# Group-norm products on GpSimd with wider stage spacing, a padded ninth tap, and late M products in a fused four-layer convolution kernel

## The chip, the cores and the metric

The kernel runs on one core of a Trainium2 chip. The metric is device time of the program in microseconds, as the median of several runs. The profile records one execution of its own: TensorE's matmuls (PE) and its weight loads (PEld), VectorE (DVE), ScalarE (ACT), GpSimd (POOL) and SyncE's DMA queue (SP).

## The reference

The input x has 4 images of 32 x 32 points and 16 channels. Four layers each add something to x. Three of them (0, 1 and 3 in the reference) are a convolution whose weights differ from point to point and whose result meets every point of the image:

```python
x = x + conv(_gn(x), M, W, G)

# conv, with L = 1
first   = einsum('ijyx,byxc->bijc', Msq, inputs)
shifted = conv3x3(inputs, kernels of all 1024 points x 16 channels)   # (b, i, j, y, x, c)
diff    = relu(inputs[:, None, None] - shifted)
second  = einsum('ijyx,bijyxc->bijc', Wsq, diff)
return first - second
```

`_gn` is a group norm over pairs of channels and the whole image. For each output point (i, j), batch and channel, `shifted` is an image of 1024 values: a product of 144 weights (9 taps by 16 channels) with the image's patches. Together that is a matrix product of 16384 rows by 144 by 4096 columns per layer. Then follow the relu and a weighted sum over the 1024 values.

Layer 2 of the reference is an interval layer: running maxima over a 32 x 32 table, then two steps that add two tables, apply a sigmoid and take a maximum, and a last small product with sigmoid.

## The kernel before

**Phases and steps.** The four images are two groups g of two (GB = 2). The kernel's three convolution layers times two groups make six phases, in the order (layer 0, g 0), (layer 0, g 1), (layer 1, g 0), and so on. While one group is in its phase, the other group's norm, transfers and splits for the next phase are done behind it. The interval layer is done behind phase 3 (for g 0) and phase 4 (for g 1).

A phase is 8 chunks t of 128 output points, and a chunk is 32 steps: 16 channels f times 2 batches b. A step computes for 128 output points and one channel an image of 2 x 512 columns in a pair of PSUM banks. There are four such pairs. `first_part` has 8 matmuls (64 rows of weights, 512 columns), then ScalarE scales the pair in place (L609); `second_part` adds 6 matmuls, then VectorE reads the pair with minimum, multiply by the row of W and sum in one instruction (`junk`, L625). `conv_layer` issues the first part of a step and then the second part of the step before. Weights and images are split into a high and a low part to keep float32's accuracy. The weights' part of that is `prep_parts`.

**Units and weights.** A unit is 4 channels of a chunk, so 8 steps. `load_raw` brings its raw weights (3 slots of 4 x 128 per partition: taps 0 to 3, taps 4 to 7, and the ninth tap), two buffers deep. `prep_parts` is a generator with 8 yields, one part for each step: VectorE masks the high part (`upper`, L175, the tile upper_w), ScalarE halves the ninth tap's weights (L151), GpSimd adds the rest to them on two slices of 32 partitions (L222), GpSimd forms the low parts WL (L224), subtracts the identity from the next unit's weights (`prep`, L185), and forms the differences WD (L212). Then SP's queue gets the next `load_raw`. The tiles of prepared weights are three deep.

**Work behind a phase.** Everything for the next phase is one generator, `behind(phase)`. Each value that it yields is the number of steps until it is resumed; IDLE (0) means: in the next step in which `prep_parts` has little to do. What a phase has not taken after its 256 steps is issued at its end in one go.

`before_conv` is the part that leads from X of the other group to its split images: `group_norm` with its stages (sums, totals of the mean, mean and difference, squares and their sums, totals of the variance, square root, reciprocal and product), a transpose on VectorE (L336), 4 transfers to DRAM (L341), 24 transfers back as shifted patches into the tile `raw` (L351), all on SP's queue, then a pause, and for each batch `split` (VectorE's `upper` of the patches, the tile upper_x; GpSimd's iz; ScalarE's iy), the halving of the ninth tap's patches on ScalarE and VectorE (L151, L154) and the differences iyz on GpSimd (L260). In the norm's totals, VectorE reduces a 32 x 32 transpose (L285, L288), adds four quarters (L294) and transposes back (L299).

`first_terms` multiplies the normed images by M: 128 matmuls (L381), two transposes (L388) and two additions to X (L391), for both groups at once. Its matrix is loaded by `load_first_terms` in two transfers (L371) into a tile with the tag `big`, which the interval layer's tables share. It is done behind phases 0, 2 and 4, after `before_conv`.

`interval_layer` has its own norm, four transposes (L464), scans in two halves each (`running`, L482) with a GpSimd copy between (L490), and then two `step`s of GpSimd additions (L536) and VectorE maxima (L543).

All instructions of an engine run in the order in which they were issued. That order is the one that these generators write out, and the schedule is by hand (`manual_schedule`).

Of the kernel before, what the change touches and what calls it, by code (L numbers as in the profile page):

```python
# [15 lines left out]
P = 128  # L16
B, H, C = 4, 32, 16
NG = 2
# [23 lines left out]
def net_kernel(ctx: ExitStack, tc: tile.TileContext, x, xq, xi, convs, iv_w, iv_b, out):  # L42
# [17 lines left out]

    nc = tc.nc
    ctx.enter_context(tc.manual_schedule())

# [30 lines left out]
    def load_raw(u):  # L96
        if u < n_chunks * NU:
            n = u // NU
            raws[u] = wpool.tile([P, 3, FU, P], F32, tag="raw", bufs=RAWS, name=f"raw_{u}")
            nc.sync.dma_start(raws[u], convs[phases[n // NT][1]][2][n % NT, u % NU])  # L100

    def load_chunk(n):
# [17 lines left out]
    plain = first[:, : PLAIN * 3 * FU * P].rearrange("p (u s f k) -> p u s f k", u=PLAIN, s=3, f=FU)  # L120
    for u in range(PLAIN):
        raws[u] = plain[:, u]
    nc.scalar.dma_start(raws[0][:, :, :F0], convs[0][2][0, 0][:, :, :F0])
    for slot in (0, 2, 1):
        nc.sync.dma_start(raw[:, slot, 0, :RUN], xi[0][:, slot, :RUN])
    load_chunk(0)
    nc.sync.dma_start(raws[0][:, :, F0:], convs[0][2][0, 0][:, :, F0:])
    nc.sync.dma_start(raw[:, :, 1, :RUN], xi[1][:, :, :RUN])
    nc.sync.dma_start(raws[1], convs[0][2][0, 1])


    eps = const.tile([P, 1], F32, name="eps")
# [58 lines left out]
    def prep_parts():  # L191

        for u in range(PLAIN, n_chunks * NU):
            units[u] = [
                wpool.tile([P, 2, FU, P], F32R, tag=tag, bufs=AHEAD + 1, name=f"{tag}_{u}")
                for tag in ("WU", "WL", "WD")
            ] + [wpool.tile([P, FU, P], F32R, tag="W9", bufs=AHEAD + 1, name=f"W9_{u}")]  # L200
            src = raws.pop(u)
            w8 = src[:, :2].rearrange("p s f k -> p s (f k)")
            w9 = src[:, 2]
            WU, WL, WD = (t.rearrange("p s f k -> p s (f k)") for t in units[u][:3])
            W9 = units[u][3]

            def scaled(s):
                nc.scalar.activation(WD[:, s], high[:, s], AF.Copy, scale=-EPS)  # L208

            def difference(s):  # L210
                nc.scalar.copy(WU[:, s], high[:, s])  # L211
                nc.gpsimd.tensor_tensor(  # L212
                    WD[:, s], WD.bitcast(F32)[:, s], WL.bitcast(F32)[:, s], ALU.add
                )

            high = upper(src[:, :2], f"w{u}")
            yield True
            halve(W9, w9, low_w)
            yield False
            scaled(0)  # L220
            for r in (slice(32, 64), slice(96, 128)):
                nc.gpsimd.tensor_tensor(W9[r], W9.bitcast(F32)[r], w9[r], ALU.add)  # L222
            for s in range(2):
                nc.gpsimd.tensor_tensor(WL[:, s], w8[:, s], high[:, s], ALU.subtract)  # L224
            yield False
            scaled(1)
            prep(u + 1)
            yield False
            difference(0)
            yield False  # L230
            difference(1)
            yield False
            load_raw(u + RAWS)
            yield True
            yield True
# [35 lines left out]
    def pair_view(ap):  # L271
        return ap.rearrange("p t (g s) -> p t g s", s=2)

    def group_norm(g, name, dst):


        def sums(src):
            nc.vector.tensor_reduce(
                part[:, : GC // 2], src.rearrange("p t (g s) -> p g t s", s=2), axis=AX.XY, op=ALU.add
            )  # L280

        def totals(name):

            turned = work.tile([P, 32], F32, tag="turned", name=f"turned_{name}")
            nc.vector.transpose(turned, part)  # L285
            by_quarter = work.tile([32, 4], F32, tag="by_quarter", name=f"by_quarter_{name}")
            for q in range(4):
                nc.vector.tensor_reduce(  # L288
                    by_quarter[:, q : q + 1], turned[32 * q : 32 * q + 32], axis=AX.X, op=ALU.add
                )  # L290
            yield 1
            total = work.tile([P, 32], F32, tag="total", name=f"total_{name}")
            for q in range(4):
                nc.vector.tensor_reduce(  # L294
                    total[32 * q : 32 * q + 32, 0:1], by_quarter, axis=AX.X, op=ALU.add
                )
            yield 1
            whole = work.tile([P, 32], F32, tag="whole", name=f"whole_{name}")
            nc.vector.transpose(whole, total[:, 0:1].to_broadcast([P, 32]))  # L299
            return whole[:, : GC // 2]  # L300

        sums(X[g])
        yield 1
        m = yield from totals(f"m{name}")
        mean = work.tile([P, GC // 2], F32, tag="mean", name=f"mean_{name}")
        nc.vector.tensor_scalar_mul(mean, m, 1.0 / (2 * NP))
        yield 1
        xc = work.tile([P, NT, GC], F32, tag="xc", name=f"xc_{name}")
        nc.vector.tensor_tensor(pair_view(xc), pair_view(X[g]), spread(mean), ALU.subtract)
        yield 1  # L310
        sq = work.tile([P, NT, GC], F32, tag="sq", name=f"sq_{name}")
        nc.vector.tensor_tensor(sq, xc, xc, ALU.mult)  # L312
        sums(sq)
        yield 1
        v = yield from totals(f"v{name}")
        yield 2
        yield IDLE
        rstd = work.tile([P, GC // 2], F32, tag="rstd", name=f"rstd_{name}")
        nc.scalar.activation(rstd, v, AF.Sqrt, bias=eps, scale=1.0 / (2 * NP))
        yield 2  # L320
        nc.vector.reciprocal(rstd, rstd)
        nc.vector.tensor_tensor(pair_view(dst), pair_view(xc), spread(rstd), ALU.mult)
        yield 2

    xns = {}
    part = const.tile([P, 32], F32, name="part")
# [2 lines left out]
    def before_conv(g, layer):  # L329
        xn = work.tile([P, NT, GC], F32, tag="xn", bufs=2, name=f"xn_{g}_{layer}")  # L330
        xns[g] = xn
        yield from group_norm(g, f"c{g}{layer}", xn)

        nc.vector.transpose(  # L336
            xt[g][:, :, 1 : 1 + H], xn
        )
        inner = xs[g][:, HP : HP + H * HP].rearrange("p (t r n) -> p r t n", r=ROWS, n=HP)
        for r in range(ROWS):  # L340
            nc.sync.dma_start(inner[:, r], xt[g][GC * r : GC * (r + 1)])  # L341
        yield 2
        xsv = xs[g].rearrange("(b c) n -> c b n", b=GB)
        at = 0
        for slot, row, tap in [(2, row, 8) for row in range(4)] + [
            (tap // 4, tap % 4, tap) for tap in range(8)
        ]:
            for h in range(2):
                off = (HI * h + tap // 3) * HP + tap % 3
                r0 = 64 * h + C * row  # L350
                nc.sync.dma_start(  # L351
                    raw[r0 : r0 + C, slot, :, :RUN], xsv[:, :, off : off + RUN]
                )
            at += 1
            if at % 3 == 0:
                yield 1
        yield 7
        for b in range(GB):
            yield from split(nc.gpsimd, g, b, f"{g}{layer}")
            yield IDLE  # L360
            halve(image(im9[g][:, b], H), image(raw[:, 2, b], HP), low_x)
            for s in range(2):
                difference(nc.gpsimd, g, b, s)
            yield 3
            halve_rest(image(im9[g][:, b], H), image(raw[:, 2, b], HP), low_x)
            yield 1
# [73 lines left out]
    def interval_layer(g):  # L440
# [14 lines left out]
        yield 1  # L455
        nc.gpsimd.memset(r[:R, :, 0:1], 0.0)
        nc.gpsimd.memset(r[:R, H:], 0.0)
        yield from group_norm(g, f"i{g}", xi)

        raw = one[:GC].rearrange("p (j t r) -> p r t j", j=H, r=ROWS)  # L460
        for row in range(ROWS):
# [16 lines left out]
        def running(dst, src):  # L478

            for half in range(2):  # L480
                o = slice(n // 2 * half, n // 2 * (half + 1))
                nc.vector.tensor_tensor_scan(  # L482
                    dst[:, o], resets[:, o], src[:, o], 0.0, op0=ALU.add, op1=ALU.max
                )
                yield 2


        yield from running(one[:, ::-1], other[:, ::-1])
        yield 1
        nc.gpsimd.tensor_copy(table(other), one.rearrange("p (j i) -> p i j", i=H))  # L490
        yield 3
        yield from running(one, other)
# [33 lines left out]
        def step(name, ftp, bias):  # L526
# [20 lines left out]
            nc.scalar.activation(s, s, AF.Sigmoid, bias=bias)  # L547
            for q in range(NQ):
                nc.sync.dma_start(r[R:, QI * q : QI * (q + 1), :], s[GC * q : GC * (q + 1)])
            yield 5  # L550

        yield from right_side("r0", iv["r0"])
        ftp = left("l0", iv["f0"])
# [117 lines left out]
    def behind(phase):  # L671
# [7 lines left out]
        if phase + 1 < len(phases):  # L679
            g1, layer1 = phases[phase + 1]  # L680
            if layer1 == 2:
                yield from interval_layer(g1)
            if g1 == NG - 1:
                mt = load_first_terms(layer1)
            yield from before_conv(g1, layer1)
            if g1 == NG - 1:
                yield from first_terms(layer1, mt)
        if phase == len(phases) - 1:
            yield 4
            nc.sync.dma_start(out[1 - g], X[1 - g])  # L690

# [114 lines left out]
    def rest_of_start():  # L806
# [22 lines left out]
        nc.vector.memset(part, 0.0)  # L829
        zeros(0)  # L830
        xns[0] = work.tile([P, NT, GC], F32, tag="xn", bufs=2, name="xn_00")
        yield from group_norm(0, "c00", xns[0])

    parts = prep_parts()
    for phase in range(len(phases)):
# [77 lines left out]
```

## Time and profile before

| What | Value |
|---|---|
| Median of 3 runs | 2612.41 us (2611.65 to 2615.23) |
| Profiled execution's own time | 2615.03 us |
| Its span | 2613.1 us |
| PE busy | 2570.9 us, 98% |
| DVE busy | 2203.8 us, 84% |
| ACT busy | 2094.6 us, 80% |
| POOL busy | 1812.9 us, 69% |
| DMA, 16 engines, q1 | 200.13 MB, 22.7% |
| Granted TensorE clock | 1.00 |

How to read it: matmuls are pipelined and their ends are modelled, so 98% for PE is not PE at its peak; the chain and the waits show where it stood still. L579 is the line of all the convolution's matmuls. In a row of the groups, the name before the arrow is the tile written, those after it are read; then come partitions x elements, the count, busy us and mean ns, and the idle time of the engine before them. The phases end (last matmul) at 450.4, 874.4, 1305.3, 1745.1, 2190.9 and 2608.7 us.

### The profile page before, as it was taken

What the parts mean: (1) busy time and instruction counts of PE and PEld (TensorE: products, weight loads), DVE (VectorE), ACT (ScalarE), POOL (GpSimd) and SP (SyncE); (2) the same over time, 40 slices, a digit from 0 to 9 for tenths busy, and PEclk for the clock granted to TensorE, in tenths of its full rate; (3) what the DMA queues carried; (4) which work ended last, traced back from release to release, by engine and by line L of the source; (5) the groups of instructions that cost most, each with busy time, mean ns of one, the idle gap of its engine ahead of it and who ended that gap; (6) DMA issues with size and microseconds to landing.
All of it is one profiled execution on the core that took longest, in us unless ns stands there. A gap on an engine that the chain in (4) does not pass through costs nothing.

```text
span 2613.1 us, 56851 instructions
## 1 busy us (share of the span) xinstructions
PE 2570.9 (98%) x21906; PEld 2034.2 (78%) x21906; DVE 2203.8 (84%) x3684; ACT 2094.6 (80%) x2549; POOL 1812.9 (69%) x1446
## 2 busy tenths in 40 slices
PE   8999999999999999999999999999999999999999
PEld 5778888778888778888877777777778778888887
DVE  9977778987787887877798899889889887787877
ACT  4778888788888778888877888877888878888886
POOL 5776666776666676666667887777878676666663
PEclk9999999999999999999999999999999999999999
DMA  3422222312222322222222212311222332222220
GB/s 131 148 82 70 69 70 78 95 68 69 70 77 70 133 87 70 77 71 68 71 68 70 71 58 72 105 69 58 70 72 73 131 95 72 70 77 71 69 70 15
DMA packets 50287, 204.36 MB, mean 78 GB/s; under 512 B 12128, under 2 KB 14048, under 8 KB 49248
## 3 DMA queue, kind: packets, MB, share of 16 engines
q1 hardware_dynamic: 49056, 200.13, 22.7%
q8 instruction: 172, 2.82, 0.4%
q14 instruction: 99, 0.81, 0.1%
q10 hardware_dynamic: 832, 0.58, 0.1%
q0 software_dynamic: 128, 0.02, 0.0%
HBM read 199.19 MB, written 0.98 MB: 77 GB/s over the span
## 4 chain that ended last, share of the span: by engine, by line
PE 88%; DVE 7%; issue 3%; ACT 1%; SPq 0%; DMA 0%; DVEq 0%; POOL 0%; POOLq 0%; ACTq 0%
PE pc L579 87%; DVE junk L625 5%; PE pf L381 1%; DVE upper_w L175 1%; ACT pc L609 0%; SPq L351 0%; DMA raw<-in_g 0%; PE ps_l L504 0%; PE ps_r L517 0%; DVE tables L464 0%; DVE by_quarter_vc L288 0%; DVE acc L638 0%; DVE sq_c L312 0%; DVE sq_i L312 0%; SPq L341 0%
## 5 line engine op out<-in xcount | busy, mean ns | idle before, releaser
L625 DVE SCALAR_TENSOR_TENSOR junk<-pc,WT 128x1024 f32<-128x1024 f32 x1536 | 1877.8, 1223 | 384.6 <-PE pc L579 337.5
L609 ACT ACTIVATE pc<-pc 128x1024 f32<-128x1024 f32 x1520 | 1531.9, 1008 | 468.8 <-PE pc L579 420.4
L579 PE MATMUL pc<-iy,WU 64*128 64x512 f32 x6080 | 970.2, 396 | 28.5 <-DVE junk L625 28.1
L222 POOL TENSOR_TENSOR W<-W,raw 32x512 fp32r<-32x512 f32 x380 | 498.6, 1312 | 708.3 <-issue 614.0
L579 PE MATMUL pc<-iyz,WD 64*128 64x512 f32 x6080 | 962.6, 393 | 2.3 <-ACT pc L609 2.3
L579 PE MATMUL pc<-iz,WL 64*128 64x512 f32 x6080 | 961.1, 392 | 0.0
L579 PEld LDWEIGHTS pc<-iy,WU 64*128 64x128 f32 x6080 | 569.4, 185 | 190.8 <-DVE junk L625 58.0
L579 PEld LDWEIGHTS pc<-iyz,WD 64*128 64x128 f32 x6080 | 575.3, 185 | 142.7 <-ACT pc L609 8.6
L579 PEld LDWEIGHTS pc<-iz,WL 64*128 64x128 f32 x6080 | 576.5, 185 | 135.3
L579 PE MATMUL pc<-im,W 64*128 64x512 f32 x3072 | 619.0, 397 | 0.0
L224 POOL TENSOR_TENSOR WL<-raw,upper_w 128x512 fp32r<-128x512 f32 x380 | 489.0, 1308 | 16.7 <-DVE upper_w L175 2.1
L212 POOL TENSOR_TENSOR WD<-WD,WL 128x512 fp32r<-128x512 f32 x380 | 491.8, 1317 | 0.0
L579 PEld LDWEIGHTS pc<-im,W 64*128 64x128 f32 x3072 | 291.6, 185 | 72.1 <-issue 3.3
L208 ACT ACTIVATE WD<-upper_w 128x512 fp32r<-128x512 f32 x380 | 236.9, 624 | 19.3 <-DVE upper_w L175 19.2
L211 ACT CAST WU<-upper_w 128x512 fp32r<-128x512 f32 x380 | 233.5, 615 | 0.0
L185 POOL TENSOR_TENSOR raw<-raw,pick 128x512 f32<-128x512 f32 x190 | 203.5, 1071 | 5.9 <-DMA raw<-in_g 5.9
L175 DVE TENSOR_SCALAR upper_w<-raw 128x1024 int32<-128x1024 int32 x190 | 160.4, 844 | 0.2
L151 ACT ACTIVATE W<-raw,low_w 128x512 fp32r<-128x512 f32 x190 | 135.9, 715 | 0.1
L625 DVE DVE_READ_ACCUMULATOR junk<-pc,WT 128x1 f32 x1536 | 127.3, 83 | 0.0
L536 POOL TENSOR_TENSOR tables<-ft_b,rt 128x1089 f32<-128x1089 f32 x16 | 37.8, 2364 | 7.4 <-ACT ft_b L529 7.4
L536 POOL TENSOR_TENSOR tables<-ft_a,rt 128x1089 f32<-128x1089 f32 x16 | 37.9, 2368 | 4.4 <-ACT ft_a L529 4.4
L579 PE MATMUL pc<-raw,first 64*128 64x512 f32 x128 | 32.2, 623 | 1.8 <-DVE raw L783 1.8
(134 smaller groups left out, 397.7 us busy)
## 6 DMA issues: line engine op xcount, KB each, us to landing
raw<-in_g SPq DMA_DIRECT2D x190, 768.0 KB, 4.3
WT<-in_w SPq DMA_DIRECT2D x48, 512.0 KB, 3.6
MT<-in_mt SPq DMA_DIRECT2D x6, 2048.0 KB, 11.1
raw<-xs SPq DMA_DIRECT2D x120, 67.8 KB, 3.0
raw<-in_xi SPq DMA_DIRECT2D x3, 271.0 KB, 4.2
raw<-in_xi SPq DMA_DIRECT2D x1, 813.0 KB, 7.5
first<-in_g SPq DMA_DIRECT2D x1, 768.0 KB, 8.1
xs<-xt SPq DMA_DIRECT2D x20, 34.0 KB, 2.2
```

The lines of the kernel that those rows point to most:

```text
L151: nc.scalar.activation(dst, src, AF.Copy, scale=mask[:, 1:2])
L175: nc.vector.tensor_scalar(t.bitcast(I32), src.bitcast(I32), HIGH, None, op0=ALU.bitwise_and)
L185: eng.tensor_tensor(raws[u][:, 1, at:to], raws[u][:, 1, at:to], pick[:, f0 + at : f0 + to].unsqueeze(2).to_broadcast([P, to - at, P]), ALU ...
L208: nc.scalar.activation(WD[:, s], high[:, s], AF.Copy, scale=-EPS)
L211: nc.scalar.copy(WU[:, s], high[:, s])
L212: nc.gpsimd.tensor_tensor(WD[:, s], WD.bitcast(F32)[:, s], WL.bitcast(F32)[:, s], ALU.add)
L222: nc.gpsimd.tensor_tensor(W9[r], W9.bitcast(F32)[r], w9[r], ALU.add)
L224: nc.gpsimd.tensor_tensor(WL[:, s], w8[:, s], high[:, s], ALU.subtract)
L536: nc.gpsimd.tensor_tensor(t, ft[:, i, :].unsqueeze(1).to_broadcast([P, T1, T1]), rt, ALU.add,)
L579: nc.tensor.matmul(ps[:, h, :], lhsT=w[r], rhs=v[r], start=first and k == 0, stop=k == len(pairs) - 1, skip_group_check=not first,)
L609: nc.scalar.activation(ps, ps, AF.Copy, scale=1.0 + EPS)
L625: nc.vector.scalar_tensor_tensor(junk, ps.rearrange("p h n -> p (h n)"), 0.0, chunks[n], op0=ALU.min, op1=ALU.mult, accum_out=accs[phase][ ...
```

## The change

It has four parts.

1. In `group_norm`, the mean, the difference xc, the squares sq and the final product move from VectorE to GpSimd, and the first three are issued together. The function gets a parameter `gap`, the number of steps between its VectorE stages: 4 before a convolution in layers 0 and 1, 1 before the last layer's convolution, 2 in the interval layer.
2. Other pauses change: 7 to 4 steps between the patches' transfers and `split`; 2 to 3 after each half of a scan, without the one step between the first two scans and the copy; 5 to 4 after a table's transfer.
3. The raw weights get a fourth slot, made on the host: the ninth tap's weights with zeros where nothing is to be added. So the addition to W9 is one instruction on 128 partitions. A raw load is 1024 KB instead of 768. The first two units, which aren't split, load three slots as before.
4. The last layer's M products go from phase 4 into phase 5: its matrix is loaded at the phase's head, and the products follow 24 steps later.

```diff
-            raws[u] = wpool.tile([P, 3, FU, P], F32, tag="raw", bufs=RAWS, name=f"raw_{u}")
+            raws[u] = wpool.tile([P, 4, FU, P], F32, tag="raw", bufs=RAWS, name=f"raw_{u}")
...
-            for r in (slice(32, 64), slice(96, 128)):
-                nc.gpsimd.tensor_tensor(W9[r], W9.bitcast(F32)[r], w9[r], ALU.add)
+            nc.gpsimd.tensor_tensor(W9, W9.bitcast(F32), src[:, 3], ALU.add)
...
-    def group_norm(g, name, dst):
+    def group_norm(g, name, dst, gap):
...
-            yield 1
+            yield gap
             total = work.tile([P, 32], F32, tag="total", name=f"total_{name}")
...
-            yield 1
+            yield gap
             whole = work.tile([P, 32], F32, tag="whole", name=f"whole_{name}")
...
         sums(X[g])
-        yield 1
+        yield gap
         m = yield from totals(f"m{name}")
         mean = work.tile([P, GC // 2], F32, tag="mean", name=f"mean_{name}")
-        nc.vector.tensor_scalar_mul(mean, m, 1.0 / (2 * NP))
-        yield 1
+        nc.gpsimd.tensor_scalar_mul(mean, m, 1.0 / (2 * NP))
         xc = work.tile([P, NT, GC], F32, tag="xc", name=f"xc_{name}")
-        nc.vector.tensor_tensor(pair_view(xc), pair_view(X[g]), spread(mean), ALU.subtract)
-        yield 1
+        nc.gpsimd.tensor_tensor(pair_view(xc), pair_view(X[g]), spread(mean), ALU.subtract)
         sq = work.tile([P, NT, GC], F32, tag="sq", name=f"sq_{name}")
-        nc.vector.tensor_tensor(sq, xc, xc, ALU.mult)
+        nc.gpsimd.tensor_tensor(sq, xc, xc, ALU.mult)
+        yield 4
         sums(sq)
-        yield 1
+        yield gap
...
         nc.vector.reciprocal(rstd, rstd)
-        nc.vector.tensor_tensor(pair_view(dst), pair_view(xc), spread(rstd), ALU.mult)
-        yield 2
+        nc.gpsimd.tensor_tensor(pair_view(dst), pair_view(xc), spread(rstd), ALU.mult)
+        yield 3
...
-        yield from group_norm(g, f"c{g}{layer}", xn)
+        yield from group_norm(g, f"c{g}{layer}", xn, 1 if layer == 2 else 4)
...
-        yield 7
+        yield 4
         for b in range(GB):
             yield from split(nc.gpsimd, g, b, f"{g}{layer}")
...
-        yield from group_norm(g, f"i{g}", xi)
+        yield from group_norm(g, f"i{g}", xi, 2)
...
-                yield 2
+                yield 3
         yield from running(one[:, ::-1], other[:, ::-1])
-        yield 1
...
-            yield 5
+            yield 4
...
-            if g1 == NG - 1:
+            terms = g1 == NG - 1 and layer1 < NL - 1
+            if terms:
                 mt = load_first_terms(layer1)
             yield from before_conv(g1, layer1)
-            if g1 == NG - 1:
+            if terms:
                 yield from first_terms(layer1, mt)
         if phase == len(phases) - 1:
+            mt = load_first_terms(layer)
+            yield 24
+            yield from first_terms(layer, mt)
             yield 4
             nc.sync.dma_start(out[1 - g], X[1 - g])
...
-        yield from group_norm(0, "c00", xns[0])
+        yield from group_norm(0, "c00", xns[0], 4)
...
-        give(f"g{n}", np.broadcast_to(g, (NT, NU, 2, 64, 3, FU, P)).reshape(NT, NU, P, 3, FU, P))
+        g = np.concatenate([g, g[:, :, :, :, 2:]], axis=4)
+        g[:, :, :, :32, 3] = 0.0
+        give(f"g{n}", np.broadcast_to(g, (NT, NU, 2, 64, 4, FU, P)).reshape(NT, NU, P, 4, FU, P))
```

More of the change, by code (lines that the diff above doesn't have):

```diff
@@ L122, in net_kernel @@
         raws[u] = plain[:, u]
-    nc.scalar.dma_start(raws[0][:, :, :F0], convs[0][2][0, 0][:, :, :F0])
+    nc.scalar.dma_start(raws[0][:, :, :F0], convs[0][2][0, 0][:, :3, :F0])
     for slot in (0, 2, 1):
@@ L126, in net_kernel @@
     load_chunk(0)
-    nc.sync.dma_start(raws[0][:, :, F0:], convs[0][2][0, 0][:, :, F0:])
+    nc.sync.dma_start(raws[0][:, :, F0:], convs[0][2][0, 0][:, :3, F0:])
     nc.sync.dma_start(raw[:, :, 1, :RUN], xi[1][:, :, :RUN])
-    nc.sync.dma_start(raws[1], convs[0][2][0, 1])
+    nc.sync.dma_start(raws[1], convs[0][2][0, 1][:, :3])
     eps = const.tile([P, 1], F32, name="eps")
```

## The prediction, made before the result was known

> **What bounds the kernel now.** I read the page first, then the chain of work that ended last in order of time, then the waits, and last the timeline of single stages.
>
> ```profile
> PE 2570.9 (98%) x21906; PEld 2034.2 (78%) x21906; DVE 2203.8 (84%) x3684; ACT 2094.6 (80%) x2549; POOL 1812.9 (69%) x1446
> 2149.84 456.85 PE pc L579 x3914
> 2142.80 7.04 PE pf L381 x128
> ```
>
> The last two lines are pieces of the chain. The first of them is the kernel at its best: 3914 matmuls in 456.85 us, 116.7 ns each. A step (one channel of one batch) has 14, so it costs 1.634 us; the 1520 steps that have 14 make 2484 us. The other 129 us of the span are the start up to step 16 (some 43), three blocks of M products (3 x 7.0), the tail after the last matmul (4), and some 60 of stalls and of the interval layer's matmuls. The waits name the stalls:
>
> ```profile
> PEld pc L579 <- DVE junk L625: 58.6, 73, 1.7
> POOL W L222 <- issue: 614.0, 157, 5.9
> ```
>
> TensorE waits 58.6 us for VectorE, 73 times, to free a PSUM bank pair. So VectorE bounds only short stretches. This is one, the norm at the head of phase 1:
>
> ```profile
> 456.49 1.76 DVE L175 TENSOR_SCALAR upper_w<-raw 128x1024 int32<-128x1024 int32 x1
> 459.45 0.73 PE L579 MATMUL pc<-iy,WU 64*128 64x512 f32 x4 [0.88 <-DVE junk L625]
> 459.55 1.24 DVE L306 TENSOR_SCALAR mean_c<-whole_mc 128x16 f32<-128x16 f32 x1
> 461.98 0.73 PE L579 MATMUL pc<-iy,WU 64*128 64x512 f32 x4 [0.64 <-DVE junk L625]
> 463.35 1.37 DVE L312 TENSOR_TENSOR sq_c<-xc_c 128x256 f32<-128x256 f32 x1
> 466.37 0.73 PE L579 MATMUL pc<-iy,WU 64*128 64x512 f32 x4 [0.86 <-DVE junk L625]
> ```
>
> VectorE gets something extra in every step. Back to back, its evictions start every 1.36 us, so it catches up 1.634 - 1.36 = 0.27 us a step; what exceeds that piles up, and with four bank pairs TensorE stops once an eviction starts some 1.7 us late (read from these stalls: evictions 2.9 and 3.8 us late gave stalls of 1.1 and 0.9).
>
> From the ends of the matmuls in the timeline I took each step's excess over 1.634 us. Steps with norm stages on VectorE: 3.2 us and 2.1 in phase 0, 4.0 in phase 1, 4.0 in phase 2, 2.95 each in phases 3 and 4 (the interval layer's own norm): **19.2 us**. The two layer-2 norms late in phases 3 and 4: 1.8 each. The scans (L482) with what falls between them: 4.7 each. Phase 5, with no work behind it, has none.
>
> **The change part by part.**
>
> *Norm products to GpSimd, stages apart.* VectorE loses mean, xc, sq and dst. By the rows of the groups (L306, L309, L312, L322: 579 + 433 + 734 + 904 ns) that is 2.65 us in each of six norms, and 3.6 in the two interval norms. What stays is two sums (0.42), two groups of transpose and four reductions (0.95), two of four reductions (0.62), two transposes (0.2). At four steps apart VectorE catches up 1.08 us between stages, more than the largest; at two steps apart the worst step has 0.95 plus upper_w (0.69), under 1.7. So I take all 19.2 us as gone. With gap 1 (layer 2) the stages still crowd; there I take 0.4 of 1.8 in each phase.
>
> On GpSimd nothing shows a 128x256 product. The nearest row is L224 (128x512, 1308 ns): half is 0.65, so with mean (0.23, as the 64x32 row of L415) a norm costs 2.2 us, 8 norms 18 us. The Trainium skill speaks against it: "GPSIMD Engine Reference", section 4.1 Engine selection, keeps two-input elementwise work on VectorE, since GpSimd is about 2x slower. By that rule, from VectorE's undisturbed 0.42, a product is 0.84 and 8 norms are 22 us; and the time would be lost where GpSimd sets the pace. Here its row has over 600 us idle, so both prices give 0 on the path. The cover is the distance: sums(sq) comes four steps (6.5 us) after the products, L336 three steps (4.9 us) after dst. In the interval norm the products queue behind WL, prep and one difference, and are still done some 4 us before VectorE asks. Without that cover, VectorE's queue stands: evictions are behind it, TensorE behind those.
>
> A second rule points the other way. "SBUF — State Buffer", section Who interferes with whom: a two-input VectorE operation on SBUF and a GpSimd operation that reads SBUF exclude each other, as do the fast tensor_scalar modes; the second one waits. The trace agrees:
>
> ```profile
> L175 DVE TENSOR_SCALAR upper_w<-raw x190: 682/690/2848, 19.5 to 2574.3; 128x1024 int32<-128x1024 int32 x190
> L222 POOL TENSOR_TENSOR W<-W,raw 32x512 fp32r<-32x512 f32 x380 | 498.6, 1312 | 708.3 <-issue 614.0
> L224 POOL TENSOR_TENSOR WL<-raw,upper_w 128x512 fp32r<-128x512 f32 x380 | 489.0, 1308 | 16.7 <-DVE upper_w L175 2.1
> ```
>
> (The first line gives min/median/max.) Of 190 upper_w, 28 are over 0.8 us, and mostly an L222 had begun just before, because VectorE was late. On time, it comes first. By the rule each moved product could in turn block an upper_w, up to 0.65 us in 8 norms (5 us of VectorE time); by the step arithmetic they fall in other steps than upper_w, so 0.
>
> *Ninth tap in one addition.* L222 is two instructions on 32 partitions at 1312 ns; L224 on 128 partitions costs 1308, so partitions are free: 190 x 1.31 = 249 us off GpSimd. It is off the path: 0, or up to 2 us through shorter locks. Its price is the raw load: 1024 KB for 768, 188 times, 48 MB more. At the row's 4.3 us that makes about 5.7 us against one load per 13.07 us, used a unit later; hidden. If it came late, prep on GpSimd would wait, behind it the differences, then upper_w on VectorE. At the start raw_2 and raw_3 land at 15.6 and 17.5 us; a third more still comes before the first upper_w at 19.5.
>
> *Scans at three steps for two.* Four scans of 1.2 to 2.2 us: two more steps in all give 0.5 us, and they leave the addition at the chunk's end (L639, 1.97 us beside a GpSimd copy) and half of the overlap with GpSimd's split work. Adding scan by scan against 0.27 a step leaves some 2.2 of 4.7: 2.5 us gained in each of two phases, **5.0** (2 to 7).
>
> *M products to the last phase.* The same 128 matmuls, 7.04 us, elsewhere: 0. The two MT loads (2048 KB each, 13.8 us to the later landing in phase 2) go into SP's queue at the head of phase 5, ahead of raw and WT loads; the next raw load is up to 13 us off and has a unit's slack. -1 to +1. The other yields (5 to 4 after a table, 2 to 3 after a norm) only shift work; counted through, the last halving of phases 3 and 4 goes from step 230 to 246 of 256 and still fits. Past 256 the rest would be issued in one heap.
>
> *Seven steps to four before split.* **This costs.** VectorE's upper_x waits for the last of 24 small transfers, which SP issues after four others, after L336. Steps between L336 and upper_x: 2 + 4 + 7 = 13 before (21.2 us), 2 + 4 + 4 = 10 after (16.3). How long the transfers take:
>
> ```profile
> 481.97 1.80 SPq L341 DMA_DIRECT2D xs<-xt  x4
> 486.58 11.59 SPq L351 DMA_DIRECT2D raw<-xs  x24
> 501.39 1.39 DVE L175 TENSOR_SCALAR upper_x<-raw 128x1024 int32<-128x1024 int32 x1
> 134.47 0.69 DVE L175 TENSOR_SCALAR upper_x<-raw 128x1024 int32<-128x1024 int32 x1 [1.32 <-DMA raw<-xs]
> ```
>
> In phase 1, L336 started at 481.50 and the last transfer landed at 500.95, 19.45 us later; in the five phases it was 19.5 to 21.7. So it is just in time now, and short by 1.32 us in phase 0. SP's issue sets it (0.47 us each). I take 19.8 after: no raw load in the new order has to wait for its buffer on SP, but one larger load falls among the 24. The wait is 19.8 - 16.3 = 3.5 us (2.2 to 5.5), behind it on VectorE the evictions, behind those TensorE. The price by the one such row: in phase 0, 1.32 us of wait and an upper_w close behind cost TensorE 0.4; without that neighbour 0.6 less, with 2.2 more wait: 2.0. The upper_w three steps later comes before the lag is caught up: 0.4 more. 5 x 2.4 - 0.4 = **11.6 us lost** (4 to 20).
>
> **Sum.** -19.2 - 0.8 - 5.0 + 11.6 = -13.4; for locks and alignments of the halving rows (L154, 1.4 to 1.9 us, now two steps after an upper_w) I give back 1.5: -12. The profiled execution took 2615.0 us, so 2603; it lies 2.6 above the median of the runs, so **2601 us** as a median.
>
> **Rivals.**
> *The transfers come in time* (chance 0.2): then the loss is 0 to 3 and the gain 22 to 28: about 2588. For it: SP is relieved of waits for buffers. Against: 28 issues at 0.47 us and two landings are 18 us already.
> *No change* (0.14): wait about 5 us in each phase, or GpSimd late at sums(sq): 5 x 4 us take back the 24, near 2610. For it: in phases 0 and 4 the chain took over 21 us.
> *Slower* (0.08): the same wait, where the larger raw load stops SP among the 24 (there are gaps of 1 to 2 us now). Each us costs 5 us. The gain of 24 is used up at 5.9 us of wait (a chain of 22.2); at 7 it is 6 us more: 2618. Against: no chain in the trace is that long.
> The forecast itself has 0.58.
>
> **Numbers.** A run tells 0.2% (5 us) from no change. Faster 0.78, same 0.14, slower 0.08. The range leaves out half of the first rival's low side and the slower case: 2586 to 2612; the forecast alone, from the ends of the losses and gains, 2594 to 2607.
>
> **What would show it.** TensorE's wait for junk falls from 58.6 to some 45; no idle rows with that name in the first 40 steps of phases 1 and 2; upper_x waits for raw<-xs five times, 3 to 4 us each; L222 has 190 of 128x512 at 1.3 us; the M products of layer 2 stand in phase 5 at 7.0 us; sums(sq) and L336 wait for nothing on GpSimd. It is wrong if upper_x does not wait, or if VectorE waits for GpSimd.

## The result, and the profile after

The changed kernel takes 2599.48 us (median of 4 runs, 2597.44 to 2601.62), against 2613.82 us for the kernel before (4 runs, 2611.65 to 2615.35). The ratio is 0.9946, with a 95% interval of 0.9929 to 0.9963: 14.3 us faster. The forecast was 2601. Its direction and size were right, and so was the one cost that it named; but several smaller terms were wrong in both directions and partly cancelled. Put back to seven steps, the pause that the change had shortened makes the same kernel another 16.6 us faster.

The profiled execution of the changed kernel took 2597.4 us, the shortest of the four, with a span of 2595.7 us for 2613.1 before. The page gives each engine's busy time, share and instructions:

```profile
PE 2561.7 (99%) x21906; PEld 2048.5 (79%) x21906; DVE 2151.6 (83%) x3652; ACT 2094.7 (81%) x2549; POOL 1564.6 (60%) x1288
```

The waits of the same kernel (us in total, times, longest):

```profile
PEld pc L577 <- DVE junk L623: 28.4, 28, 3.4
...
DVE upper_x L176 <- DMA raw<-xs: 19.3, 5, 4.7
```

GpSimd is 248 us less busy, VectorE 52. TensorE waits for VectorE 28 times instead of 73. And there is a new row: VectorE waits five times, once in each phase but the last, for the patches.

Where the norm of phase 1 had TensorE idle four times, the timeline of the changed kernel has no such row. GpSimd's timeline there:

```profile
472.47 0.25 POOL L306 TENSOR_SCALAR mean_c<-whole_mc 128x16 f32<-128x16 f32 x1 [7.88 <-DVE whole_mc L299]
472.81 0.68 POOL L308 TENSOR_TENSOR xc_c<-X,mean_c 128x256 f32<-128x256 f32 x1
473.57 0.61 POOL L310 TENSOR_TENSOR sq_c<-xc_c 128x256 f32<-128x256 f32 x1
474.14 1.30 POOL L222 TENSOR_TENSOR W<-W,raw 128x512 fp32r<-128x512 f32 x1
```

The three products and the one addition of the ninth tap run one after another. GpSimd stood idle for 7.9 us before them, waiting for VectorE's `whole_mc`; TensorE loses nothing in these steps.

The chain of work has the M products of the last layer in phase 5 now, with TensorE in one piece on both sides:

```profile
2118.31 87.09 PE pc L577 x742
2205.40 7.04 PE pf L380 x128
2212.44 376.81 PE pc L577 x3228
```

The place that costs is split. The transfers of phase 1 on SP's queue, then VectorE's and TensorE's rows:

```profile
515.11 1.81 SPq L340 DMA_DIRECT2D xs<-xt  x4
518.87 2.63 SPq L350 DMA_DIRECT2D raw<-xs  x6
521.61 0.36 SPq L101 DMA_DIRECT2D raw<-in_g  x1
522.01 10.09 SPq L350 DMA_DIRECT2D raw<-xs  x18
...
534.04 0.69 DVE L176 TENSOR_SCALAR upper_x<-raw 128x1024 int32<-128x1024 int32 x1 [2.98 <-DMA raw<-xs]
...
535.93 0.73 PE L577 MATMUL pc<-iy,WU 64*128 64x512 f32 x4 [1.31 <-DVE junk L623]
```

From the first of the four transfers to upper_x it is 18.9 us; before the change it was 19.0 from there (481.97) to the last landing (500.95). VectorE comes for it three steps earlier and stands 2.98 us; TensorE then finds no free bank pair for 1.3.

In phase 2 VectorE stands 4.69 us and TensorE 3.01, and more follows. TensorE's rows there, and then two stretches of the profile with PE's busy time, the granted clock, and DMA:

```profile
957.60 1.22 PE L577 MATMUL pc<-iy,WU 64*128 64x512 f32 x4 [3.01 <-DVE junk L623]
958.62 1.05 PE L577 MATMUL pc<-iz,WL 64*128 64x512 f32 x4
960.69 0.63 PE L577 MATMUL pc<-iy,WU 64*128 64x512 f32 x4
961.16 0.63 PE L577 MATMUL pc<-iz,WL 64*128 64x512 f32 x4
...
957.20:960.60 3.40, 3.00 (x14) 0.50 0.19 80
961.00:964.40 3.40, 3.40 (x32) 1.00 0.21 39
```

For 3.4 us the granted clock is 0.50 instead of 1.00, and four matmuls take 1.05 us instead of 0.63. The same happens in phase 0, from 213.1 us, behind a stall of 2.83. It does not happen behind the stalls of phases 1, 3 and 4 (1.31, 2.50 and 2.27 us). At half the clock, matmuls end every 212 ns instead of 116.5, so by estimate the two stretches cost 1.5 and 1.4 us.

The steps' excess over 1.634 us, read from the ends of the matmuls as in the prediction, gives the account (us, after minus before, from the two profiled executions):

| Where | Change |
|---|---|
| Norm stages, phases 0 to 4 (18.8 before) | -18.8 |
| Layer-2 norms (1.8 to 0.6 each) | -2.3 |
| Transposes before the scans (0.8 each, now none) | -1.6 |
| Scans (4.7 to 3.2 each) | -2.9 |
| Additions and maxima of the tables (4.7 to 2.2 in all) | -2.5 |
| Halving rows after split (8.0 to 1.3 in all) | -6.7 |
| Two one-off steps of phase 0 | -1.4 |
| Wait for the patches, five phases, with some 2.9 of halved clock | +15.6 |
| Small mask operation in phase 0 | +2.1 |
| Start of the kernel | +1.2 |
| M products: 7.24 out of phase 4, into phase 5 | 0 |
| Sum (the spans differ by 17.4) | -17.3 |

The medians differ by less, 14.3 us: the other three executions of the changed kernel ran at a mean granted clock of 0.997 or 0.998, the profiled one at 0.999, and the runs of the kernel before whose clock is on record at 0.999 or 1.000.

### The profile page after: what moved, and what is told of

The parts are those of the page before. It is cut to its first block, busy times and chain, and to the rows that moved or that the text cites. A ratio compares the mean times of both kernels' runs of the same rounds, so it can differ in the third digit from the quotient of the medians.

```text
span 2595.7 us, 56475 instructions
## 1 busy us (share of the span) xinstructions
PE 2561.7 (99%) x21906; PEld 2048.5 (79%) x21906; DVE 2151.6 (83%) x3652; ACT 2094.7 (81%) x2549; POOL 1564.6 (60%) x1288
## 4 chain that ended last, share of the span: by engine, by line
PE 92%; DVE 3%; DMA 2%; issue 2%; SPq 1%; ACT 1%; DVEq 0%; ACTq 0%
PE pc L577 91%; DVE junk L623 2%; SPq L350 1%; PE pf L380 1%; DMA raw<-in_g 1%; DMA raw<-xs 1%; ACT pc L607 0%; DMA xs<-xt 0%; SPq L340 0%; DVE upper_w L176 0%; PE ps_l L502 0%; DMA XQ<-in_xq 0%; DVE s_b L541 0%; PE ps_r L515 0%; DVE xt L335 0%
## 5 line engine op out<-in xcount | busy, mean ns | idle before, releaser
L222 POOL TENSOR_TENSOR W<-W,raw 128x512 fp32r<-128x512 f32 x190 | 250.7, 1320 | 832.1 <-ACT W L152 829.0
L577 PEld LDWEIGHTS pc<-iy,WU 64*128 64x128 f32 x6080 | 577.0, 185 | 162.4 <-DVE junk L623 27.2
L176 DVE TENSOR_SCALAR upper_w<-raw 128x1024 int32<-128x1024 int32 x190 | 140.2, 738 | 0.1
L253 POOL TENSOR_TENSOR iz<-raw,upper_x 128x512 fp32r<-128x512 f32 x20 | 23.8, 1202 | 23.2 <-DVE upper_x L176 23.2
```

What stands on the lines that cost most here:

```text
L176: nc.vector.tensor_scalar(t.bitcast(I32), src.bitcast(I32), HIGH, None, op0=ALU.bitwise_and)
L222: nc.gpsimd.tensor_tensor(W9, W9.bitcast(F32), src[:, 3], ALU.add)
L577: nc.tensor.matmul(ps[:, h, :], lhsT=w[r], rhs=v[r], start=first and k == 0, stop=k == len(pairs) - 1, skip_group_check=not first,)
```

## The experiments

**Theory:** the norms' gain is real, and the shorter pause gives back some 15 us of it. **Rivals:** the pause only uses slack; and, inside the norms, the gain comes from the engine, or from the distance.

**1. The pause alone, put back.**

```diff
-        yield 4
+        yield 7
         for b in range(GB):
             yield from split(nc.gpsimd, g, b, f"{g}{layer}")
```

> The changed kernel with the pause before split back at 7 steps. Theory (the shorter pause costs 11 to 16 us: VectorE waits 19.3 us in five upper_x for raw<-xs, and TensorE loses 16 us in the steps behind them): upper_x waits under 2 us in all, TensorE's stalls behind it go, 2585 us (2581 to 2590). Rival (the wait is slack that comes back at another place, since the later half of split is then as close to the phase's work as before): no change, 2596 to 2603 us.

Measured: 2582.87 us, ratio to the kernel before 0.9886 (0.9870 to 0.9903). The wait for the patches is gone from its waits, and TensorE waits 18.6 us for VectorE:

```profile
PEld pc L577 <- DVE junk L623: 18.6, 29, 1.9
```

The shorter pause costs 16.6 us between the medians and 14.4 between the profiled executions. Step by step, 16.1 us go at the five waits, the halved clock with them, and 2.0 come back in the halving rows behind split, which stand better with the shorter pause. The granted clock is 1.00 throughout the phases here.

**2. The same edit in the kernel before.**

```diff
-        yield 7
+        yield 4
```

> The kernel before with the one edit that costs: 4 steps for 7 before split. Theory (upper_x comes 4.9 us earlier and the patches do not; before, it waited 1.3 us in phase 0 and was 0 to 1.3 us late in the others): waits of 3.6 to 6.2 us, 24 us in all, less 1 us of slack each: 2632 us (2626 to 2638). Rival (TensorE and VectorE have that slack in the kernel before): 2612 to 2618 us.

Measured: 2632.70 us, ratio 1.0071 (1.0056 to 1.0087), 18.9 us slower:

```profile
PEld pc L579 <- DVE junk L625: 68.0, 66, 4.4
...
DVE upper_x L175 <- DMA raw<-xs: 24.8, 5, 5.6
```

The waits were worked out as 24 us from landing times and steps, and are 24.8. That the shorter pause makes these waits, and costs 17 to 19 us in either kernel, stands from both sides. How the 18.9 come about was not foreseen. The steps at the five waits lose 26.4 us, and behind each of them the granted clock is 0.50 for 3.4 us (6.8 in phase 1), some 8.7 us by the estimate above; the halving rows behind split give 6.7 back (8.0 to 1.3 us). The theory had neither, so that its number was met is partly luck.

**3. Products back on VectorE.**

```diff
-        nc.gpsimd.tensor_scalar_mul(mean, m, 1.0 / (2 * NP))
+        nc.vector.tensor_scalar_mul(mean, m, 1.0 / (2 * NP))
```

and likewise for xc, sq and the last product.

> The changed kernel with mean, xc, sq and the last product of the norm back on VectorE, all distances kept. Theory (the distance between the stages carries the gain of the norms, not the engine): VectorE has 2.6 us more in a norm, but 1.2 us in one step and 0.7 in another, within the lag that TensorE allows: 2602 us (2599 to 2607), no stall of more than 1 us in the norms. Rival (the engine carries it): most of the 19 us of the norms come back, 2611 to 2619 us.

Measured: 2612.49 us (12 runs, 2605.96 to 2617.57), as the rival said. VectorE's rows in phase 1, and below them those of GpSimd and TensorE at the same time:

```profile
475.40 1.47 DVE L308 TENSOR_TENSOR xc_c<-X,mean_c 128x256 f32<-128x256 f32 x1
476.90 1.15 DVE L310 TENSOR_TENSOR sq_c<-xc_c 128x256 f32<-128x256 f32 x1
...
474.04 2.55 POOL L224 TENSOR_TENSOR WL<-raw,upper_w 128x512 fp32r<-128x512 f32 x2
476.54 1.23 POOL L186 TENSOR_TENSOR raw<-raw,pick 128x512 f32<-128x512 f32 x1
...
479.25 0.73 PE L577 MATMUL pc<-iy,WU 64*128 64x512 f32 x4 [0.98 <-DVE junk L623]
```

Operations of 0.42 us take 1.47 and 1.15 while GpSimd reads SBUF. Three of them in one step, and TensorE stalls: 1.25 us in phases 1 and 2, 1.9 in phase 0, 3.2 in each layer-2 norm, 10.8 in all. My theory had the durations of undisturbed operations. The wait for the patches takes 2 us more than in the changed kernel.

**4. All stages one step apart, products on GpSimd.**

```diff
-        yield from group_norm(g, f"c{g}{layer}", xn, 1 if layer == 2 else 4)
+        yield from group_norm(g, f"c{g}{layer}", xn, 1)
...
-        yield 4
+        yield 1
         sums(sq)
```

and gap 1 in the other two calls.

> The changed kernel with all norm stages one step apart again (gap 1 everywhere, and one step between the products and their sums), the products still on GpSimd. Theory (distance carries the gain): VectorE still has a stage in every step, and waits for GpSimd's products besides: 2612 us (2606 to 2620), with VectorE waiting for sq. Rival (the engine carries it): 2597 to 2603 us.

Measured: 2612.13 us (12 runs, 2606.81 to 2619.48). The time fits the theory, the profile does not: the steps of the norm in phase 1 lose 0.8 us, not 4. What grew is the wait for the patches, 22.1 us, one of 5.6. TensorE loses 22.6 us in the steps at these waits, 6.5 more than in the changed kernel, and its clock was halved for 17 us in all (6.8 in the changed kernel). So 3 and 4 could not tell engine from distance by their times, because a changed norm also shifts everything behind it against the transfers. I tried both again on the version of experiment 1, where upper_x does not wait.

**5. Gap 1 with the longer pause.**

> The version with a pause of 7 steps before split (2582.9 us; no wait for the patches), with all norm stages one step apart, the products on GpSimd. It takes the wait of upper_x out of the question that the earlier run with gap 1 left open. Theory A (moving the products off VectorE is most of the gain of the norms; in the earlier run with gap 1 the steps of the norms lost only about 0.5 us each): 2588 us (2585 to 2592). Theory B (distance is most of it): the 19 us of the norms return but for 2 to 5, 2597 to 2602 us.

Measured: 2592.63 us (2591.57 to 2594.32), 9.8 above experiment 1: just past the upper end of theory A and below B. VectorE does wait for GpSimd's squares, as the prediction priced without the cover:

```profile
DVE part L278 <- POOL sq_c L310: 3.4, 6, 0.6
...
DVE part L278 <- POOL sq_i L310: 1.2, 2, 0.6
```

That is 0.6 us each time, for VectorE. In the profiled execution, which is the longest of the four (11.3 above that of experiment 1), TensorE loses 1.2 us more in phase 1 and 0.8 in phase 2; the norm's own steps have 0.8 of it in each, where all of them lost 4.0 in the kernel before. Some of the rest of phase 1 is a wait for the patches, 0.6 us on VectorE: it is small here, but not gone. Phases 3 and 4 lose 2.7 to 2.9 each, largely in later work that stands in other steps. Phase 0 loses 3.9, of which some 1.5 is clock: behind a stall of 1.82 us the granted clock was 0.50 for 3.4 us from 79.4.

**6. Products on VectorE, each in a step of its own, with the longer pause.**

```diff
+        nc.vector.tensor_scalar_mul(mean, m, 1.0 / (2 * NP))
+        yield gap
...
+        nc.vector.tensor_tensor(pair_view(xc), pair_view(X[g]), spread(mean), ALU.subtract)
+        yield gap
...
+        nc.vector.tensor_tensor(sq, xc, xc, ALU.mult)
+        sums(sq)
```

> The version with a pause of 7 steps, with the products back on VectorE, each in a step of its own, a gap apart (4 in layers 0 and 1, 2 in the interval layer, 1 in layer 2). The earlier run with the products on VectorE had three of them in one step, and there GpSimd stretched xc from 0.42 to 1.47 us and sq to 1.15. Theory C (distance alone is enough once the products do not share a step): 2586 us (2583 to 2590). Theory D (the products have to leave VectorE, since GpSimd's additions stretch them): 2592 to 2600 us.

Measured: 2591.00 us (2589.80 to 2591.40), 8.1 above experiment 1, between C and D. Phases 1 and 2 lose 1.0 and 0.3 us only, and that not in the norm's steps but in the halving rows. Phases 3 and 4 lose 3.0 each, in the layer-2 norm, which has gap 1. TensorE's rows there:

```profile
1628.08 0.73 PE L578 MATMUL pc<-iy,WU 64*128 64x512 f32 x4 [0.28 <-DVE junk L624]
1632.46 0.73 PE L578 MATMUL pc<-iy,WU 64*128 64x512 f32 x4 [0.86 <-DVE junk L624]
1634.63 0.73 PE L578 MATMUL pc<-iy,WU 64*128 64x512 f32 x4 [0.27 <-DVE junk L624]
```

From 5 and 6: either half of the edit alone removes most of a norm's stall (in phase 1 the norm's steps lost 4.0 us before, 0.8 with the move alone, none with the distance alone). Where steps are plentiful, distance is enough; in the crowded norm, the move is what helps. Their gains do not add up.

**7. Ninth tap as before, in the changed kernel.**

```diff
-            nc.gpsimd.tensor_tensor(W9, W9.bitcast(F32), src[:, 3], ALU.add)
+            for r in (slice(32, 64), slice(96, 128)):
+                nc.gpsimd.tensor_tensor(W9[r], W9.bitcast(F32)[r], w9[r], ALU.add)
```

with three slots again in the load.

> The changed kernel with the ninth tap as before: raw loads of 768 KB and two additions on 32 partitions. Theory (GpSimd is off the path): POOL busy up by 249 us, the raw load back at 4.3 us, time 2600 us (2596 to 2604). A part of the wait of upper_x may go with the smaller load: at most 1 us in each of five phases. Rival (relief of GpSimd carries part of the gain, by shorter locks of upper_w): 2605 to 2615 us.

Measured: 2598.90 us, the same as the changed kernel within its runs. GpSimd is 260 us busier than in the changed kernel, by the page:

```profile
PE 2565.5 (99%) x21906; PEld 2048.5 (79%) x21906; DVE 2170.3 (84%) x3652; ACT 2095.5 (81%) x2549; POOL 1824.8 (70%) x1478
```

and, from its waits:

```profile
DVE upper_x L176 <- DMA raw<-xs: 17.0, 5, 3.8
```

Several effects cancel. Phases 3 and 4 are 4.1 us longer each, phases 0 to 2 are 5.8 shorter together. Part of both is the clock: its two halved stretches stand in phases 3 and 4 here (from 1683.3 and 2120.2 us) and in phases 0 and 2 in the changed kernel, some 1.5 us each. Without them phases 3 and 4 lose 2.6 each, and the five waits cost some 2.4 us less than in the changed kernel, with 17.0 us on VectorE for 19.3.

**8. The same with the longer pause.**

> The version with a pause of 7 steps, with the ninth tap as before (raw loads of 768 KB, two additions on 32 partitions). In the run on the changed kernel this cost 4 us in each of phases 3 and 4 and gained 9 in phases 0 to 2, most of it in the wait of upper_x. Theory (with no wait left, only the cost remains): 2591 us (2587 to 2595). Rival (GpSimd is off the path, and the 4 us were the run's own): 2580 to 2586 us.

Measured: 2588.85 us (2588.54 to 2589.38), 6.0 above experiment 1. The groups of upper_w, first in this kernel and then in that of experiment 1:

```profile
L176 DVE TENSOR_SCALAR upper_w<-raw 128x1024 int32<-128x1024 int32 x190 | 158.8, 836 | 0.1
```

```profile
L176 DVE TENSOR_SCALAR upper_w<-raw 128x1024 int32<-128x1024 int32 x190 | 146.0, 769 | 0.1
```

VectorE's masks cost 13 us more beside the longer GpSimd work. Nearly all of the 6 us is in phases 3 and 4 (2.7 each), mostly in steps with the tables' maxima and an upper_w. So GpSimd's load is not free, though GpSimd is idle for 29% of the span.

**9. Scans as before, with the longer pause.**

```diff
-                yield 3
+                yield 2
         yield from running(one[:, ::-1], other[:, ::-1])
+        yield 1
```

> The version with a pause of 7 steps, with the scans two steps apart and one step before the copy, as before. Theory (three steps gained 2.5 us in each of phases 3 and 4; they still lose 2.9 there): 2587 us (2585 to 2590). Rival (the gain in these phases was the norm's alone): 2581 to 2585 us.

Measured: 2594.02 us, 11.2 above experiment 1, more than either said. But the steps of the scans lose what they lost at three steps, 2.9 us in a phase (the 2.2 in the next expectation leaves out one step of 0.65). The loss is in later work: steps with the tables' maxima, the sigmoid and the layer-2 norm stall 1.1 to 1.5 us where they stalled up to 0.8 or not at all, 5.3 us in each of phases 3 and 4. The work right behind the scans had moved by three steps against upper_w, which comes every eight, and some of what follows by six or eight.

**10. Scans as before, later work in its place.**

```diff
             fill=0.0, base=0, channel_multiplier=0,
         )
-        yield 5
+        yield 8
```

> The version with a pause of 7 steps, with the scans two steps apart and one before the copy as before, and the three steps that this saves added after the scans, so that all later work keeps its place in the 8 steps of a unit. Theory (in the run with scans at two steps the scans themselves lost less, 2.2 us for 2.9 in a phase; the 11 us came from the later work, which moved against upper_w): 2582 us (2579 to 2585). Rival (the distance of the scans is what counts): 2590 to 2596 us.

Measured: 2582.27 us (2581.33 to 2582.56). With the three steps added after the scans, the 11 us are gone, and the steps of the scans still lose 2.9 us in a phase. The distance of the scans is worth nothing; the place of the later work in the unit's eight steps is worth 11 to 12 us (11.2 from experiment 1 to 9, 11.8 from 9 to 10).

**11. M products back in phase 4.**

```diff
-            terms = g1 == NG - 1 and layer1 < NL - 1
+            terms = g1 == NG - 1
```

and without the load and the products at the head of phase 5.

> The version with a pause of 7 steps (2582.9 us), with the last layer's M products back in phase 4. Theory (128 matmuls cost TensorE 7.24 us wherever they stand, and the loads of M hit nothing in either place): 2583 us (2581 to 2585), 7.2 us gone from phase 5 and back in phase 4. Rival (the loads of M in SP's queue ahead of the patches, or the end of phase 4, cost something): 2586 to 2592 us.

Measured: 2583.36 us (2582.77 to 2584.29), for 2582.87: no difference between the medians. In the profiled executions phase 5 is 7.2 us shorter, phase 4 is 9.7 longer, and the start, which the edit does not touch, is 1.1 shorter. So phase 4 pays 2.5 us beyond the products, 2.0 of it in one step that comes well before them, behind this upper_w:

```profile
2115.28 4.42 DVE L176 TENSOR_SCALAR upper_w<-raw 128x1024 int32<-128x1024 int32 x1
...
2115.31 2.59 POOL L260 TENSOR_TENSOR iyz<-iy,iz 128x512 fp32r<-128x512 f32 x2
2117.82 1.33 POOL L222 TENSOR_TENSOR W<-W,raw 128x512 fp32r<-128x512 f32 x1
```

In experiment 1 the same upper_w began 1 us after iyz, not 0.03 before it, and took 0.88 us. Whether the edit or chance made the difference, one profile of each does not show.

**12. The mask operation moved, on top of 10.** In the changed kernel, GpSimd's and VectorE's timelines around a one-time operation of phase 0 are these:

```profile
109.64 1.06 POOL L167 DMA_DIRECT2D xs<-zero  x2
110.72 2.52 POOL L213 TENSOR_TENSOR WD<-WD,WL 128x512 fp32r<-128x512 f32 x2
113.17 1.02 POOL L421 MEMSET rt<- 128x1089 f32 x1
...
110.40 3.81 DVE L409 TENSOR_SCALAR mask<-mask 32x2 f32<-32x2 f32 x1
```

It took 0.16 us in the kernel before.

```diff
             zeros(1)
-            yield 1
+            yield 3
...
         nc.gpsimd.memset(rt, 0.0)
-        yield 1
+        yield 7
```

> The version with a pause of 7 steps and the scans of the last run, with two steps more between the zeros of the second image buffer and the constants, and six more behind the constants' memset, so that all later work keeps its place in a unit. In the changed kernel the small mask operation L409 (32x2) took 3.8 us where it took 0.16 before, behind an unbroken row of GpSimd work, and TensorE lost 2.1 us. Theory (the step decides): L409 back under 0.5 us, 2580 us (2578 to 2582). Rival (the loss is that of the constants, wherever they stand): 2581.5 to 2584 us.

Measured: **2580.32 us** (2579.67 to 2580.60), ratio to the kernel before 0.9874 (0.9858 to 0.9891). L409 takes 0.58 us there, a little over the 0.5 expected, and TensorE's 2.1 us are gone. This is the fastest of all versions, 32.6 us under the kernel before and 19 under the changed one.

## Why the prediction was right, point by point

*What bounds the kernel.* Right: the pace of TensorE is the same, 116.7 ns a matmul, and nearly all that moved was stalls behind VectorE. The prediction has no term for the granted clock, which fell to 0.50 behind two of the new stalls.

*Norm products and distances.* Right in its sum: 19.2 us said, 18.8 gone (in phase 0, 1.46 us of the first step of the norm belong to the start, and are still there). Its reason needs more care: I argued from distance, with the move as relief. Experiments 5 and 6 show that either alone does most. GpSimd's price was right: 18 us said, 17.9 in the groups (0.68, 0.61, 0.68 and 0.25 us a norm). By the rule of the Trainium skill ("GPSIMD Engine Reference", 4.1 Engine selection) it was 22; a product's 0.61 to 0.68 us for 0.42 on VectorE is about 1.5 to 1.6 times, not 2, and either price was covered by idle time. The other rule, of mutual exclusion on SBUF, matters from the other side: that the moved products block no upper_w to speak of was right (all 190 take 140.2 us for 160.4), but experiment 3 shows products that stay on VectorE stretched from 0.42 to 1.47 us beside GpSimd. The layer-2 norm was undersized: 0.4 said, 1.15 gained.

*Ninth tap at 0, up to 2.* In the changed kernel its gain is hidden by what the larger load and the clock do (experiment 7). Without the wait for patches it is worth 6.0 us (experiment 8). The step that failed is "it is off the path": GpSimd's idle time is true as an average, but VectorE's masks meet GpSimd's operations, and in phases 3 and 4 VectorE has little slack. A reading led there: of the 28 long upper_w in the kernel before, only 13 stand beside the ninth tap's L222; 8 stand beside iyz (L260) and 6 beside the tables' additions (L536).

*Scans, 5.0.* The table gives 2.9, and experiment 10 says that the distance earned none of it; what did earn it, no run isolates. The failed step is the scan-by-scan sum: it looked at the scans alone, and not at what the edit does to the place of all later work.

*M products at 0.* Right by the medians (experiment 11), with one step of phase 4 left open there.

*Seven to four.* Right in mechanism and sign, with its place and its five waits: 3.5 us each said, 3.9 measured, because the transfers took 20.2 us on average for 19.8. 11.6 us said, 15.6 by the steps, 16.6 between the medians of experiment 1. The mis-sized term is what follows a wait: TensorE lost 4.6 us in each of phases 0 and 2. About 2.9 us of the whole is the halved clock behind those two stalls, which the prediction lacked; what is left, 12.7 us, is close to what it said.

*The correction for halving rows.* It had the wrong sign: 1.5 us to give back, 6.7 gained. I had added up that an upper_w comes two steps before a halving row. What changed is upper_x: it no longer meets a long piece of GpSimd work, and takes 0.69 us in every phase for up to 1.64 before. The halving rows themselves are still stretched (1.3 to 1.9 us). That it is a matter of place is shown: the shorter pause alone, in the kernel before (experiment 2), takes these rows from 8.0 to 1.3 us. The tables' additions and the transposes before the scans, which I did not price, gained 4.1 in phases 3 and 4; no run isolates them, though experiment 9 shows that such work reacts to its place.

*What would show it.* TensorE's wait for junk was to fall to 45 us and fell to 28, largely for these same unpriced gains.

So the forecast's 2601 was good to 1.5 us partly by luck: in the profiled executions the gains were some 13 us larger than said (36.2 for 23.5) and the losses 7 (18.9 for 11.6), and the other executions of the changed kernel were slower than the profiled one.

## What to carry to other kernels

An average idle share says who has time, not when: price an engine's work at the steps where another one meets it. When a schedule is written in steps, an edit that changes a count of steps also moves all work behind it, so compare it with a version in which the later work keeps its place. And a pause ahead of a wait is sized by the transfers' own chain (here 28 issues on one queue and two landings, 19 to 21 us): three steps less cost 17 us. A stall of TensorE can cost more than its length: look at the granted clock in the microseconds behind it.

## What the runs showed of the hardware that was not expected

A VectorE operation of 32x2 values took 3.81 us instead of 0.16. It began while GpSimd was issuing its DMAs, and ended only with a memset, after two additions, all of which GpSimd started later, at 110.72 and 113.17 us: by these rows it did not get its turn between them. The upper_w of experiment 11 went the same way, with 4.42 us for 0.69 in a row of three GpSimd operations. In the section that the prediction named of "SBUF — State Buffer", the Trainium skill has one side wait for the other's instruction; here it waited through an unbroken row of them.

The granted TensorE clock reacts to stalls of a few us. In the 14 profiles it falls to 0.50 in 17 places inside the phases, for 3.4 or 6.8 us, and each time the fall begins between 1.0 us before and 1.4 us after the end of a TensorE stall of 1.8 us or more. 14 other stalls of 1.5 us or more have none behind them, so the length alone does not decide. The five profiles without a stall of 1.5 us (the kernel before and experiments 1, 6, 8 and 12) have no fall.

This is also why the kernels with the wait for the patches are less steady: 2606 to 2619 us over 12 runs each in experiments 3 and 4, against 1 to 3 us between the fastest and the slowest of four runs in each version with the longer pause. The times go with the run's mean granted clock. In experiment 3 the four runs at 0.999 took 2606.0 to 2612.7 us and the three at 0.995 or 0.996 took 2615.3 to 2617.6; in experiment 4 the longest, 2619.5 us, is the one at 0.994.
